# Fewer transfers for the same bytes: left slabs by two each, and both column halves of z by one

## The chip, the core and the metric

The kernel runs on one core of one Trainium2 chip. Its metric is device time in microseconds (us). The core has five engines that run side by side: TensorE (PE in the profile; PEld is its loading of weights), VectorE (DVE), ScalarE (ACT), GpSimd (POOL) and SyncE (SP), whose queue here issues nearly all DMA transfers. The transfers themselves are carried by 16 DMA engines that all queues share.

## The reference

An image x of 512 x 512 positions with 64 channels goes through two layers of the same form. A layer is

```
x = x + conv(groupnorm(x))               # 32 groups of 2 channels over the whole image

def conv(x):                             # DIM 64, HID 128, WIN 4, n = 512
    xn    = layernorm(x)
    left  = (xn @ Wl + bl) * mask * sigmoid(xn @ Wlg + blg)
    right = (xn @ Wr + br) * mask * sigmoid(xn @ Wrg + brg)
    gate  = sigmoid(xn @ Wog + bog)
    out   = sum over d in -4..4 of left[i, i + d] * right[i + d, j]     # for all j, per channel
    out   = layernorm(out) * gate
    return out @ Wo + bo
```

So `left` is needed only near the diagonal, in a band nine wide, and for each of the 128 channels the band times `right` is a banded matrix product along the rows. The second layer needs the group statistics of the whole first output.

## The kernel before

**Tiling.** The rows are cut in nine overlapping blocks of 64 (`S`, line 23; `row_blocks`, line 146), each with a halo of 4 rows. A block gives 56 finished rows, or 60 at the two edges of the image. The 512 columns are taken as two halves of 256 (`LH`, line 172) that are worked on together: partitions 0 to 63 hold the 64 rows at a column of the left half, partitions 64 to 127 the same rows at the matching column of the right half. A *unit* (class `Unit`, line 505) is 8 columns (`JU`) of each half, so its tile `z` has 128 partitions and 8 x 64 values, 2 KB a partition. Eight units make a chunk of 64 columns, four chunks a block: 36 chunks and 288 units in each layer.

**Stages of a unit.** `load` (line 514) brings z from the image. Two transfers do this, one for each column half (lines 520 and 521): 64 rows of 2 KB. GpSimd scales and moves it by the group norm (`scaled`, `moved`), VectorE takes the row statistics (`inner_stats`), GpSimd centres and rescales (`centred`, `rescaled`), TensorE turns it (`transposed`) and ScalarE keeps both turned copies. TensorE then projects to `right` and its gate; ScalarE and VectorE finish that into the tile RO. Once the eight units of a chunk are there, `mix` (line 720) multiplies the band matrices with RO, 16 channels at a time (`HA`, line 28). Sixteen units later (`LAG`) the second half of the work follows: statistics of the output, `norm` on GpSimd or ScalarE, turns and gates on TensorE, the product with Wo, the residual from tile XR, which `fetch` (line 876) loads again from the image, and `stored` (line 909). In the first layer the result goes to `mid_x` in HBM, in the second to the output.

**Left slabs.** The values near the diagonal are computed once a layer and lie in HBM. For each block `spread_left` (line 678) lays them out in `left_of`, again in HBM, as band matrices with zeros beside the band. `take_left` (line 706) brings one slab of them into the tile A: for one group `h` of 16 channels, 128 partitions of 8 x 128 values. It does so by four transfers of 128 KB: for each half `e` of the partitions two transfers of 4 x 512 B a partition. There are eight groups, and a slab is taken anew for every block, so 72 slabs a layer. Taking starts in the `load` step of a later unit, once the last chunk of the block before has used the slab (`on_copy`, line 1095, puts it in the list `slabs`; `on_load`, line 977, takes one from it).

**Order.** The order of the work is written out by hand in the tables FIRST (line 39) and SECOND (line 69), for the first and the second layer. A word such as `load:15` means: do the load step of unit 15, counted from the start of the period. One pass over the table is a period of eight units. Each engine gets its instructions in the order of the table and works through them in order (the class `InOrder`, line 488, is why the profile shows nearly everything at line 496). So the SP queue holds, in one line, the loads of z, the slabs of A, the fetches of XR, and the stores; an issue that waits holds up those behind it. z has 12 buffers (`NZ`, line 30), XR six. A load of z waits until the unit that used its buffer 12 units ago is turned. At the start of a layer 12 units are loaded ahead of the rest.

In SECOND the loads stand in bunches: `load:15`, `load:16`, `load:12` and `load:14` follow each other within four lines, and `load:19`, `load:17`, `load:18` within another four. Their `scale` steps come a few lines later. In FIRST they are spaced more evenly.

Of the kernel before, what the change touches and what calls it, by code (L numbers as in the profile page):

```python
# [20 lines left out]
WIN = 4  # L21
NEAR = 2 * WIN + 1
S = 64
JC = 64
JU = 8
JQ = 4
NU = JC // JU
HA = 16
# [130 lines left out]
def tile_two_banded_layers(  # L159
# [8 lines left out]
    H = layers[0]["Wl"].shape[1]  # L168
# [3 lines left out]
    LH = L // 2  # L172
# [15 lines left out]
    span = 2 * (S + 2 * WIN)  # L188
    size = S * H // 2 * span
    left_of = dram.tile([2, size], F32, name="left_of")  # L190
# [86 lines left out]
    def strided(v: bass.AP, at: int, *dims) -> bass.AP:  # L277

        return bass.AP(tensor=v.tensor, offset=v.offset + at, ap=[list(d) for d in dims])


    def fetch_layer(i: int, w: dict, tmp) -> dict:
# [9 lines left out]
        for e in range(2):  # L292
            part = slice(e * D, (e + 1) * D)
            for n, nm in enumerate(("r", "rg", "l", "lg", "og")):
                load(f["raw"][part, n * H : (n + 1) * H], w[f"W{nm}"])
            load(f["ns"][part], col(w["norm_scale"]))
            load(f["nb"][part], col(w["norm_bias"]))
# [207 lines left out]
    class Unit:  # L505
# [4 lines left out]
        def __init__(self, at: int, blk: Block = None, j: int = 0, near: int = None):  # L510
            self.at, self.blk, self.j, self.near = at, blk, j, near
            self.pr, self.sg, self.banks = {}, {}, {}

    def load(src: bass.AP, u: Unit):
        u.z = zp.tile([P, JU, D], F32, tag=f"z{u.at % NZ}", name="z")
        if u.near is not None:
            load_near(src, u)
            return
        rows = slice(u.blk.s, u.blk.s + S)
        for e, j in enumerate((u.j, LH + u.j)):  # L520
            en.sync.dma_start(u.z[e * S : (e + 1) * S], src[rows, j : j + JU, :])

    def load_near(src: bass.AP, u: Unit):
        spans = [(0, u.near, u.near + JU)]
        if u.near + JU > NEAR * JQ:
            spans = [(o, u.near, u.near + JQ) for o in range(0, JU, JQ)]
        for o0, n0, n1 in spans:
            for o, r, k, m in runs(n0, n1):
                z = u.z[:, o0 + o : o0 + o + m, :].rearrange("q m c -> q (m c)")
                at, q0, q1 = r * (L + 1) + k - WIN, 0, P  # L530
                pieces = []

                if r == 0 and k < WIN:
                    q0, g = 1, min(m, WIN - k)
                    pieces = [(0, 0, g, 0), (0, g, m, at + g)]
                if r == JQ - 1 and k + m > WIN + 1:
                    q1, g = P - 1, max(0, WIN + 1 - k)
                    end = (P - 1) * JQ * (L + 1) + at
                    pieces = [(P - 1, 0, g, end), (P - 1, g, m, L * L - m)]
                cut = [q0, *([16] if q0 else []), *([P - 16] if q1 < P else []), q1]  # L540
                for a0, a1 in sorted(zip(cut, cut[1:]), key=lambda c: c[0] - c[1]):
                    en.sync.dma_start(
                        z[a0:a1],
                        strided(
                            src, (a0 * JQ * (L + 1) + at) * D, (JQ * (L + 1) * D, a1 - a0),
                            (1, m * D),
                        ),
                    )
                for q, g0, g1, a in pieces:
                    if g0 < g1:  # L550
                        en.sync.dma_start(
                            z[q : q + 1, g0 * D : g1 * D],
                            strided(src, a * D, (D, 1), (1, (g1 - g0) * D)),
                        )
# [151 lines left out]
    def take_left(n: int, h: int):  # L706

        held[h] = n
        q = HA // 4
        for e in range(2):  # L710
            for k in range(2):
                en.sync.dma_start(
                    A[e * S : (e + 1) * S, h, k * q : (k + 1) * q].rearrange("p h i t -> p h (i t)"),
                    strided(
                        left_of, n % 2 * size + (h * HA // 2 + k * q) * span + 2 * WIN,
                        (H // 2 * span, S), (span, q), (1, 2 * S),
                    ),
                )

    def mix(c: int, h: int, b: str) -> tuple:  # L720

# [203 lines left out]
    def layer(src: bass.AP, dst: bass.AP, w: dict, stats: bool, then=None):  # L925
# [51 lines left out]
        def on_load(n, t, alt, b):  # L977
            if slabs:
                take_left(*slabs.pop(0))
            if t in units and t not in early:  # L980
                load(src, units[t])
# [106 lines left out]
        def on_band(n, t, alt, b):  # L1088
            if chunk(t):
                c, h = chunk(t)  # L1090
                while held.get(h) != c // per:
                    take_left(*slabs.pop(0))
                mixed[t] = mix(c, h, b)
# [141 lines left out]
    A = keep.tile([P, H // HA, HA // 2, S, 2], F32, name="A")  # L1235
# [38 lines left out]
def build(arrays):  # L1274
    import concourse.bacc as _bacc

    nc = _bacc.Bacc("TRN2", target_bir_lowering=False, num_devices=1)
    aps = {}
    for name in _INS:
        a = arrays[f"in_{name}_dram"]  # L1280
        aps[name] = nc.dram_tensor(
            f"in_{name}_dram", a.shape, mybir.dt.from_np(a.dtype), kind="ExternalInput"
        ).ap()
    out = nc.dram_tensor("out_0_dram", aps["x"].shape, F32, kind="ExternalOutput").ap()
    layers = [{n: aps[f"L{i}_conv_{n}"] for n in _NAMES} for i in range(2)]
    with tile.TileContext(nc) as tc:
        tile_two_banded_layers(tc, aps["x"], layers, out)
    return nc
# [10 lines left out]
```

## Time and profile before

| | us |
|---|---|
| median of 3 runs | 4308.89 |
| lowest and highest | 4305.12 and 4312.75 |
| profiled execution | 4288.38 |
| its span, first to last instruction | 4286.6 |

The profile is of one execution. Its page gives, for each engine, how long it was busy:

```profile
PE 3756.5 (88%) x94986; PEld 3258.3 (76%) x94986; DVE 3657.6 (85%) x9915; ACT 3181.7 (74%) x5976; POOL 3620.0 (84%) x4962
...
q1 hardware_dynamic: 692212, 580.43, 47.0%
```

The first line is busy time in us, its share of the span, and the count of instructions. The second is the DMA queue that SP feeds: packets, MB, and the time that its packets took as a share of 16 engines' span. A packet is one contiguous piece that a DMA engine moves, or a small record of a few bytes.

Other views are used below. The view of waits lists who waited for whom, with the total in us, the number of times and the longest one. The view of windows gives the busy time of each engine in a stretch of time, with the granted TensorE clock, the mean DMA share and GB/s. The timeline lists instructions in order of time: start and duration in us, the engine (SPq is SP's queue), what it writes and reads, and how many were merged into the row. In all of them "z<-mid_x" means that z is written from mid_x; "z<-z,ga" is the scaling of z.

### The profile page before, as it was taken

How to read it: one execution, taken by the hardware profiler on the slowest of the kernel's cores; microseconds unless marked ns; L12 is line 12 of the kernel's file. 1: busy time of each engine (PE TensorE's matmuls, PEld its weight loads, DVE VectorE, ACT ScalarE, POOL GpSimd, SP SyncE). 2: the span in 40 equal slices, each digit the busy share in tenths (PEclk: the TensorE clock that was granted, in tenths of full speed). 3: DMA queues.
4: the chain of work that ended last, by engine and by line, in shares of the span. 5: the costliest groups of instructions: out<-in, count | busy, mean ns of one | idle time of the engine just before them, and what ended most of it. 6: DMA issues, size and time to landing. Idle time of an engine off the chain costs nothing.

```text
span 4286.6 us, 223301 instructions
## 1 busy us (share of the span) xinstructions
PE 3756.5 (88%) x94986; PEld 3258.3 (76%) x94986; DVE 3657.6 (85%) x9915; ACT 3181.7 (74%) x5976; POOL 3620.0 (84%) x4962
## 2 busy tenths in 40 slices
PE   0169898989899999999995798999999999999998
PEld 0058787878788888888784687878878787878786
DVE  8988787878788888888877798989889898989897
ACT  0048787878787777878773687878888888989896
POOL 2389898989898989999855698998989898989893
PEclk9989999999999999999997899999999999999999
DMA  9843545454545444545434344444454545454533
GB/s 397 318 110 102 140 118 140 114 139 118 142 113 141 122 128 122 136 121 137 129 103 110 97 137 132 136 136 135 132 139 132 141 131 146 128 147 123 157 111 101
DMA packets 695719, 596.26 MB, mean 139 GB/s; under 512 B 138310, under 2 KB 549990, under 8 KB 692420
## 3 DMA queue, kind: packets, MB, share of 16 engines
q1 hardware_dynamic: 692212, 580.43, 47.0%
q8 instruction: 748, 12.26, 1.2%
q14 instruction: 247, 2.02, 0.2%
q0 software_dynamic: 2512, 1.56, 0.1%
HBM read 436.71 MB, written 149.74 MB: 137 GB/s over the span
## 4 chain that ended last, share of the span: by engine, by line
PE 58%; DVE 12%; POOL 9%; DMA 7%; SPq 6%; issue 5%; ACT 2%; DVEq 0%; POOLq 0%; ACTq 0%
PE banks L496 44%; PE bank L496 10%; POOL z L496 6%; SPq L496 6%; POOL on L496 3%; PE acc L496 3%; DVE sti L496 2%; DMA z<-in_x_dram 2%; DVE RO L496 2%; DVE sto L496 2%; DVE gn_st L496 2%; DMA z<-mid_x 2%; DVE XR L496 1%; DVE ZH L496 1%; ACT on L496 1%
## 5 line engine op out<-in xcount | busy, mean ns | idle before, releaser
L496 POOL TENSOR_SCALAR on<-RO,rs,nm 128x128 f32<-128x128 f32 x2520 | 1117.9, 456 | 193.3 <-PE banks L496 139.9
L496 ACT ACTIVATE on<-RO,nm,rs 128x128 f32<-128x128 f32 x2088 | 971.7, 499 | 108.4 <-PE banks L496 95.1
L496 PE MATMUL banks<-pack,ZT 64*128 64x128 f32 x9216 | 987.4, 287 | 24.4 <-DVE RO L496 15.3
L496 PE MATMUL banks<-pack,zT 64*128 64x128 f32 x9216 | 945.0, 279 | 2.2 <-issue 1.3
L496 POOL TENSOR_TENSOR z<-z,ga 128x512 f32<-128x512 f32 x556 | 649.8, 1175 | 301.9 <-DMA z<-in_x_dram 135.3
L496 ACT ACTIVATE sg<-banks 128x512 f32<-128x512 f32 x1170 | 696.1, 596 | 279.9 <-PE banks L496 253.8
L496 PEld LDWEIGHTS banks<-pack,ZT 64*128 64x128 f32 x9216 | 771.5, 194 | 148.4 <-DVE RO L496 49.6
L496 DVE TENSOR_TENSOR RO<-banks,sg 128x512 f32<-128x512 f32 x1152 | 777.6, 683 | 94.8 <-ACT sg L496 72.5
L496 DVE BATCH_NORM_STATS2 sto<-RO 128x6 f32<-128x256 f32 x2304 | 847.9, 413 | 6.7 <-ACT RO L496 2.6
L496 DVE SCALAR_TENSOR_TENSOR ZH<-banks,pack,ZH 128x896 f32<-128x896 f32 (+1 forms) x576 | 668.7, 1161 | 195.5 <-PE banks L496 163.2
L496 PEld LDWEIGHTS banks<-pack,zT 64*128 64x128 f32 x9216 | 754.0, 194 | 3.9 <-ACT zT L496 2.4
L496 PEld LDWEIGHTS banks<-RO,A 64*64 64x64 f32 x36864 | 617.2, 136 | 139.0 <-DVE RO L496 43.9
L496 PE MATMUL banks<-RO,A 64*64 64x64 f32 x36864 | 693.4, 223 | 32.3 <-issue 18.8
L496 PE MATMUL bank<-pack,ZH 128*64 128x64 f32 x18432 | 666.7, 226 | 12.5 <-DVE XR L496 5.6
L496 ACT COPY RO<-banks 128x1024 f32<-128x1024 f32 x540 | 540.2, 1008 | 173.6 <-PE banks L496 162.1
L496 POOL TENSOR_TENSOR z<-z,gb 128x512 f32<-128x512 f32 x556 | 651.5, 1177 | 3.3
L496 PEld LDWEIGHTS bank<-pack,ZH 128*64 128x64 f32 x18432 | 594.0, 139 | 72.9 <-issue 31.0
L496 ACT ACTIVATE ZH<-banks 128x896 f32<-128x896 f32 (+1 forms) x576 | 531.6, 929 | 135.2 <-PE banks L496 129.4
L496 POOL TENSOR_TENSOR z<-z,rs 128x512 f32<-128x512 f32 x586 | 611.9, 1053 | 20.9 <-DVE rs L496 20.5
L496 POOL TENSOR_TENSOR z<-z,sti 128x512 f32<-128x512 f32 x586 | 617.8, 1067 | 7.7 <-DVE sti L496 7.7
L496 PE MATMUL banks<-ZT,pack 64*128 64x448 f32 (+1 forms) x2304 | 587.3, 583 | 3.4 <-issue 1.2
L496 PE MATMUL banks<-ident,on 64*128 64x64 f32 x9216 | 461.7, 230 | 125.7 <-POOL on L496 119.3
(204 smaller groups left out, 4188.7 us busy)
## 6 DMA issues: line engine op xcount, KB each, us to landing
z<-in_x_dram SPq DMA_DIRECT2D x576, 128.0 KB
A<-left_of SPq DMA_DIRECT2D x576, 128.0 KB
z<-mid_x SPq DMA_DIRECT2D x576, 128.0 KB
gn_x<-in_x_dram SPq DMA_DIRECT2D x16, 4096.0 KB
XR<-in_x_dram SPq DMA_DIRECT2D x448, 112.0 KB
mid_x<-XR SPq DMA_DIRECT2D x448, 112.0 KB
XR<-mid_x SPq DMA_DIRECT2D x448, 112.0 KB
out_dram<-XR SPq DMA_DIRECT2D x448, 112.0 KB
```

What stands on the lines that cost most here:

```text
L496: return lambda *a, **k: tc.keep_in_program_order(f(*a, **k))
```

## The change

Two kinds of transfers are cut in fewer pieces. The bytes that are moved, where they come from and where they go stay the same, and so do all other instructions and the two tables.

```
+    def halves(v: bass.AP, j: int) -> bass.AP:
+
+        return v.rearrange("p (e l) c -> e p l c", e=2)[:, :, j : j + JU, :].rearrange(
+            "e p j c -> e p (j c)"
+        )
+
     def load(src: bass.AP, u: Unit):
...
         rows = slice(u.blk.s, u.blk.s + S)
-        for e, j in enumerate((u.j, LH + u.j)):
-            en.sync.dma_start(u.z[e * S : (e + 1) * S], src[rows, j : j + JU, :])
+        en.sync.dma_start(u.z, halves(src[rows], u.j))
...
     def take_left(n: int, h: int):
 
         held[h] = n
-        q = HA // 4
         for e in range(2):
-            for k in range(2):
-                en.sync.dma_start(
-                    A[e * S : (e + 1) * S, h, k * q : (k + 1) * q].rearrange("p h i t -> p h (i t)"),
-                    strided(
-                        left_of, n % 2 * size + (h * HA // 2 + k * q) * span + 2 * WIN,
-                        (H // 2 * span, S), (span, q), (1, 2 * S),
-                    ),
-                )
+            en.sync.dma_start(
+                A[e * S : (e + 1) * S, h].rearrange("p h i t -> p h (i t)"),
+                strided(
+                    left_of, n % 2 * size + h * HA // 2 * span + 2 * WIN,
+                    (H // 2 * span, S), (span, HA // 2), (1, 2 * S),
+                ),
+            )
```

For z, `halves` views the 64 rows of the image as an array of two column halves x 64 rows x 512 values, in that order of its dimensions, and one transfer of 256 KB writes all 128 partitions of the tile from it. Each layer has 288 of these in place of 576. The loads of the diagonal's own values (`load_near`) stay as they were.

For A, the two transfers of 4 x 512 B a partition become one of 8 x 512 B, for each half of the partitions: 144 transfers of 256 KB a layer in place of 288 of 128 KB.

## The prediction

> **What bounds the kernel now.** I read the page first, for the shares of the chain and the packets.
>
> ```profile
> span 4286.6 us, 223301 instructions
> ...
> DMA packets 695719, 596.26 MB, mean 139 GB/s; under 512 B 138310, under 2 KB 549990, under 8 KB 692420
> ...
> PE 58%; DVE 12%; POOL 9%; DMA 7%; SPq 6%; issue 5%; ACT 2%; DVEq 0%; POOLq 0%; ACTq 0%
> ```
>
> TensorE carries most of the chain that ends last; DMA and the SP queue together have 13%. The wait view then says which transfers are late.
>
> ```profile
> POOL z L496 <- DMA z<-in_x_dram: 135.3, 44, 6.7
> POOL z L496 <- DMA z<-mid_x: 114.5, 52, 10.8
> ```
>
> Columns: total us, times, longest. GpSimd scales every z after its load, and 96 of 576 loads are waited for already. So z has little spare time before its use, and a later landing is paid at once. No row of that view has TensorE waiting for A. Last I read the stretches of the input statistics and of the two layers, with the DMA share (mean of the 16 engines) and GB/s in the last two columns.
>
> ```profile
> core 0: us, PE busy (x) PEld busy (x) DVE busy (x) ACT busy (x) POOL busy (x), PEclk, DMA share, GB/s
> 0.00:150.00 150.00, 18.81 (x36) 9.26 (x36) 131.14 (x417) 1.28 (x1) 55.50 (x133) 1.00 0.96 383
> 266.00:2190.00 1924.00, 1794.33 (x47296) 1582.62 (x47298) 1597.71 (x4301) 1493.60 (x2752) 1735.71 (x2379) 0.97 0.47 126
> 2350.00:4200.00 1850.00, 1740.18 (x43682) 1509.12 (x43684) 1639.27 (x4376) 1542.30 (x2955) 1663.35 (x2196) 0.97 0.46 133
> ```
>
> In both layers TensorE is busy 93 to 94% of the time and GpSimd 90%; the 16 DMA engines less than half. As a whole, DMA is no bound. The question is whether it stays spread over 16 engines.
>
> **How transfers are spread.** The packets tell.
>
> ```profile
> z<-in_x_dram SPq DMA_DIRECT2D x576, 128.0 KB
> A<-left_of SPq DMA_DIRECT2D x576, 128.0 KB
> z<-mid_x SPq DMA_DIRECT2D x576, 128.0 KB
> ...
> XR<-in_x_dram SPq DMA_DIRECT2D x448, 112.0 KB
> mid_x<-XR SPq DMA_DIRECT2D x448, 112.0 KB
> XR<-mid_x SPq DMA_DIRECT2D x448, 112.0 KB
> out_dram<-XR SPq DMA_DIRECT2D x448, 112.0 KB
> XR<-in_x_dram SPq DMA_DIRECT2D x128, 120.0 KB
> mid_x<-XR SPq DMA_DIRECT2D x128, 120.0 KB
> XR<-mid_x SPq DMA_DIRECT2D x128, 120.0 KB
> out_dram<-XR SPq DMA_DIRECT2D x128, 120.0 KB
> ...
> left_of<-left_rows SPq DMA_DIRECT2D x64, 72.0 KB
> left_of<-A SPq DMA_DIRECT2D x8, 72.0 KB
> ```
>
> Of the 138310 packets under 512 B, the 72 slab spreads explain 72 x 1024 = 73728 (72 KB in runs of 72 B). The other 64582 are far more than there are transfers; I read them as one closing packet for each engine that took part. If every transfer used 16 engines, the rows above alone would need (1728 + 1792 + 512 + 72) x 16 = 65664: too many. If the engines taken are the largest number up to 16 that divides the leading count of the transfer (14 for 56 rows, 15 for 60, 16 for 64 or 16), they need 27648 + 25088 + 7680 + 1152 = 61568, and 3014 are left for the rarer transfers. The second fits. So here the leading count decides how many engines work on a transfer.
>
> **The change, part by part.** *z.* Today each half load leads with 64 rows on both sides: 16 engines, 4 rows of 2 KB each. The new transfer writes 128 partitions, but its source is read as 2 halves x 64 rows x 2 KB: it leads with 2. Two engines is the only count over 1 that divides both 2 and 128. I forecast that each z runs on two engines, the same two each time, 131072 B on each. No row of before shows a transfer whose two sides lead with such different counts, so this is the step that can fall. [...]
>
> Price of one z on such an engine: in the first 150 us the engines stream at 383 / (16 x 0.96) = 24.9 GB/s, which gives 5.26 us; in the second layer a busy engine moves 133 / (16 x 0.46) = 18.1 GB/s and in the first 126 / (16 x 0.47) = 16.8, which give 7.24 and 7.80 us. A mean over short transfers holds their starts; 64 rows in one go are nearer to the stream. I take 5.26 and keep 7.24 and 7.80 as the other end.
>
> The same two engines still carry a sixteenth of everything else. First layer: 0.47 x 1924 = 904 us busy, less z's 288 x 16384 B at 16.8 GB/s = 281, leaves 623 us, 2.16 us a unit (288 units). Second: 0.46 x 1850 = 851 less 261 leaves 590, 2.05 a unit. So each of the two needs 7.42 and 7.31 us a unit, where the layers now take 1924/288 = 6.68 and 1850/288 = 6.42. **The floor** of the loss, were the two never idle, is 0.74 x 288 + 0.89 x 288 = 213 + 256 = 469 us: 4758 for this execution.
>
> They are idle at times, as the loads come in bunches. The SP queue in one period (8 units) of the second layer:
>
> ```profile
> 3045.73 6.28 SPq L496 DMA_DIRECT2D z<-mid_x  x8
> ...
> 3057.25 1.09 SPq L496 DMA_DIRECT2D z<-mid_x  x2
> ...
> 3059.48 3.38 SPq L496 DMA_DIRECT2D z<-mid_x  x4
> ...
> 3083.12 1.75 SPq L496 DMA_DIRECT2D z<-mid_x  x2
> ```
>
> and GpSimd's first use of them:
>
> ```profile
> 3050.54 2.33 POOL L496 TENSOR_TENSOR z<-z,ga 128x512 f32<-128x512 f32 x2
> 3055.48 1.16 POOL L496 TENSOR_TENSOR z<-z,ga 128x512 f32<-128x512 f32 x1 [0.84 <-DMA z<-mid_x]
> 3073.21 1.17 POOL L496 TENSOR_TENSOR z<-z,ga 128x512 f32<-128x512 f32 x1
> ```
>
> Eight half loads (units 15, 16, 12, 14 of the table) go out from 3045.73, two (unit 19) at 3057.25, four (17, 18) at 3059.48: seven units within 17 us. On two engines they need 7 x 7.31 = 51.2 us, to 3096.9. Unit 18 is wanted at 3073.21, so GpSimd comes 23.7 us late; unit 14, fourth of the bunch, is wanted at 3055.48 and lands at 3045.73 + 29.2 = 3074.9. GpSimd works in order, and behind a stalled scaling stand its norms, for which TensorE's turns wait, so the period stretches. TensorE's idle 6% of a 51 us period (8 x 6.42) can take back 3 us. Net 21 x 36 periods = +756. What follows a bunch is one load, so no backlog passes on.
>
> The first layer issues its loads more evenly; there I take the floor, 8 x 0.74 = 5.9 a period, and half a load, 2.6, for idle spells: 8.5 x 36 = +306. The 12 loads ahead of each layer take 12 x 5.26 = 63 us on two engines, partly beside other work: +15 each, between 0 and 60. Sum: 4288 (span 4286.6 and what lies around it) + 306 + 756 + 30 = 5380.
>
> *A.* Each slab half is now one transfer of 64 rows x 8 x 512 B instead of two: it still leads with 64, 16 engines. The price of an issue:
>
> ```profile
> L496 SPq DMA_DIRECT2D z<-in_x_dram x592: 246/588/1962, 166.9 to 2136.8; - x198
> L496 SPq DMA_DIRECT2D A<-left_of x576: 573/614/1848, 254.4 to 4057.6; - x192
> ```
>
> (ns: shortest, median, longest.) 288 A issues fewer at 614 and 576 z issues fewer at 588 take 177 + 339 = 516 us off SP. Where z is late that buys nothing, since SP then waits as well; I count 0, between 0 and the chain's SPq share, 6% or 257 us. A slab lands later behind z on two engines, but it is loaded a chunk ahead of its use: nothing.
>
> The median run is 0.48% above the profiled one: 5380 x 1.0048 = 5406, so **5400 us**.
>
> **The rivals.**
> *Dear packets and a blocked queue.* At 7.80 us a z the first layer needs 9.96 a unit, +3.28 x 288 = 945; at 7.24 the second needs 7 x 9.29 = 65.0 a bunch, 37.5 late less 3, x 36 = 1242; with 30 that is 6505, as a median 6540. For it: busy engines show that rate now, and SP waits for transfers to land:
>
> ```profile
> SPq L496 <- DMA mid_x<-XR: 207.2, 137, 3.6
> ```
>
> so a slow z can hold the stores and fetches queued behind it. Against it: that rate is one of short pieces beside 15 other busy engines.
>
> *Two engines, but another pair each time.* Then no engine is overfull and only the landing is later, by 5.26 less 0.66 (16 KB at 24.9) = 4.6 us. Paid once a bunch in the second layer (36 x 4.6 = 166) and at each of the 44 waits of the first (202): 4309 + 368 = 4680. Nothing in the profile shows how engines are picked.
>
> *The transfer is dealt by its 128 destination partitions*, 16 engines as now. This ends on the other side: one issue less ahead of the landing, 0.59 us at each of 96 waits, 57 us, gives 4250; it decides wherever the source's leading 2 doesn't count. Against it: the spread of packets above follows the leading count, and 2 can't be cut in 16. [...]
>
> *No effect*, because z has time: the 96 waits speak against it.
>
> **How the numbers follow.** Forecast, two fixed engines near 5.3 us: 0.64. Dear packets: 0.19. Changing pair: 0.06. Sixteen engines: 0.09, of which 0.07 faster and 0.02 within the bound. No effect: 0.02. The range goes from the floor (4758 x 1.0048 = 4780) up to 6250, three quarters of the way to the dear case, and leaves out the sixteen engines, no effect, the pair case and about half of the dear one: some 2 in 10. A measurement of this kernel can tell about 0.2% from no change. Faster 0.07, same 0.04, slower 0.89.
>
> **What would show it.** With two engines, z's closing packets fall from 1152 x 16 to 576 x 2 and A's lose 288 x 16, so the hardware queue's packets fall by 17280 + 4608 = 21888; with sixteen for z only by 9216 + 4608 = 13824. GpSimd's waits for z grow from 250 us to about a thousand, TensorE's wait for GpSimd with them, most in the second layer; the mean DMA share falls below 0.4 although two engines are full. GpSimd's and TensorE's busy times stay. If z's waits shrink, the two-engine step is wrong; if they grow by under 469 us, the pairs change or an engine is faster than 24.9 GB/s.

## The result and the profile after

The changed kernel takes 5794.96 us (median of 4 runs, 5786.81 to 5802.83), the kernel before 4310.82 us beside it. The ratio is 1.344, with a 95% interval of 1.340 to 1.347: slower by 34%. The forecast was 5400 us, with a range of 4780 to 6250.

The page of the changed kernel, its lines on busy time, the DMA queue and the chain that ended last:

```profile
span 5801.1 us, 221803 instructions
...
PE 4067.7 (70%) x94986; PEld 3486.6 (60%) x94986; DVE 3691.0 (64%) x9915; ACT 3202.2 (55%) x5976; POOL 3624.2 (62%) x4962
...
q1 hardware_dynamic: 670324, 580.34, 34.5%
...
PE 28%; DMA 23%; POOL 21%; issue 13%; SPq 7%; DVE 6%; ACT 2%; POOLq 0%; DVEq 0%; ACTq 0%
```

GpSimd, VectorE and ScalarE do the same work in the same busy time, in a span that is a third longer. DMA has gone from 7 to 23% of the chain, GpSimd from 9 to 21%. Yet the queue's packets keep 16 engines busy only 34.5% of the time, where they had 47.0%: less DMA work at once, and more waiting for it.

The hardware queue has 670324 packets where it had 692212: 21888 fewer, which is what two engines for z give (18432 - 1152 closing packets less) with A's 4608. They are all under 512 B: the page counts 138310 packets of that size before and 116422 after. Sixteen engines for z would have left 678388.

A window shows the two engines themselves. Between 197 and 215 us little but loads ahead of the first layer is under way (columns as before; the last two are DMA share and GB/s):

```profile
197.00:215.00 18.00, 1.37 (x4) 1.00 (x4) 16.21 (x63) 0.00 (x0) 0.86 (x1) 1.00 0.13 49
```

0.13 of 16 is two engines on the mean, and 49 GB/s is 24.5 GB/s on each. So 131072 B take 5.35 us, where nothing else moves. The landings in the trace agree: each z leaves two landing marks after one at its issue, and four z have their last mark at 203.52, 208.87, 214.21 and 219.57, 5.34 to 5.36 us apart.

The view of waits, after, and below it the row on XR of the kernel before:

```profile
POOL z L496 <- DMA z<-mid_x: 900.4, 165, 31.8
POOL z L496 <- DMA z<-in_x_dram: 840.4, 164, 14.5
...
DVE XR L496 <- DMA XR<-mid_x: 542.4, 34, 26.0
```

```profile
DVE XR L496 <- DMA XR<-mid_x: 74.1, 11, 10.6
```

GpSimd's waits for z have gone from 250 to 1741 us, by 1491; the kernel lost 1484. XR, whose transfers were not changed, is waited for 542 us where it was 74. Its 56 or 60 rows are spread over 14 or 15 engines (as many landing marks a transfer, after one at its issue). I read it to have shares on the same two: of the 14 marks of the fetch issued at 1514.69 us, twelve came 2.0 to 2.5 us after the issue, the last two after 8.87 and 9.27 us, at 1523.56 and 1523.96; the z issued ahead of it, at 1509.83, had landed at 1522.17.

Where the time went by stages is read from the first and the last transfer of a kind. First the kernel before, then the changed one, in the view of the tile mid_x (issue in ns, then first and last start in us):

```profile
L496 SPq DMA_DIRECT2D mid_x<-XR x576: 307/436/1802, 342.3 to 2294.4; - x192
L496 SPq DMA_DIRECT2D XR<-mid_x x576: 306/394/2266, 2416.5 to 4271.0; - x192
```

```profile
L496 SPq DMA_DIRECT2D mid_x<-XR x576: 313/448/5048, 400.3 to 3025.8; - x192
L496 SPq DMA_DIRECT2D XR<-mid_x x576: 306/392/5890, 3193.8 to 5787.4; - x192
```

The first layer's stores took 1952 us and now take 2626: +673. The second layer's fetches took 1855 and now take 2594: +739. The start lost 58 us and the passage between the layers 46.

### The profile page after: what moved, and what is told of

It is laid out like the page before. It is cut to its first block, busy times and chain, and to the rows that moved or that the text cites. A ratio compares the mean times of both kernels' runs of the same rounds, so it can differ in the third digit from the quotient of the medians.

```text
span 5801.1 us, 221803 instructions
## 1 busy us (share of the span) xinstructions
PE 4067.7 (70%) x94986; PEld 3486.6 (60%) x94986; DVE 3691.0 (64%) x9915; ACT 3202.2 (55%) x5976; POOL 3624.2 (62%) x4962
## 2 busy tenths in 40 slices
DMA packets 673820, 596.08 MB, mean 103 GB/s; under 512 B 116422, under 2 KB 528102, under 8 KB 670532
## 3 DMA queue, kind: packets, MB, share of 16 engines
q1 hardware_dynamic: 670324, 580.34, 34.5%
## 4 chain that ended last, share of the span: by engine, by line
PE 28%; DMA 23%; POOL 21%; issue 13%; SPq 7%; DVE 6%; ACT 2%; POOLq 0%; DVEq 0%; ACTq 0%
PE banks L496 21%; POOL z L496 14%; DMA z<-mid_x 11%; DMA z<-in_x_dram 8%; SPq L496 7%; POOL on L496 7%; PE bank L496 5%; PE acc L496 2%; DVE gn_st L496 1%; DMA mid_x<-XR 1%; DVE ZH L496 1%; DVE RO L496 1%; ACT on L496 1%; ACT RO L496 1%; DVE XR L496 0%
## 5 line engine op out<-in xcount | busy, mean ns | idle before, releaser
L496 POOL TENSOR_TENSOR z<-z,ga 128x512 f32<-128x512 f32 x556 | 650.4, 1170 | 1823.2 <-DMA z<-mid_x 900.4
L496 PE MATMUL banks<-ident,on 64*128 64x64 f32 x9216 | 541.5, 243 | 845.4 <-POOL on L496 839.5
L496 PE MATMUL banks<-pack,ZT 64*128 64x128 f32 x9216 | 1056.5, 301 | 108.0 <-DVE RO L496 98.4
L496 PEld LDWEIGHTS banks<-ident,on 64*128 64x128 f32 x9216 | 427.6, 150 | 972.8 <-POOL on L496 911.3
L496 PE MATMUL banks<-pack,zT 64*128 64x128 f32 x9216 | 1002.9, 290 | 2.5 <-issue 1.6
L496 PEld LDWEIGHTS banks<-pack,ZT 64*128 64x128 f32 x9216 | 841.0, 208 | 239.6 <-DVE RO L496 120.2
L496 DVE TENSOR_TENSOR XR<-bank,XR 120x512 f32<-120x512 f32 (+1 forms) x576 | 391.9, 680 | 813.5 <-DMA XR<-mid_x 542.4
L496 PEld LDWEIGHTS banks<-pack,zT 64*128 64x128 f32 x9216 | 812.6, 206 | 2.9 <-ACT zT L496 2.1
L496 DVE BATCH_NORM_STATS2 sti<-z 128x6 f32<-128x128 f32 x2344 | 505.7, 281 | 459.5 <-POOL z L496 456.7
L496 PE MATMUL bank<-pack,ZH 128*64 128x64 f32 x18432 | 723.6, 237 | 34.3 <-DVE XR L496 25.5
L496 PEld LDWEIGHTS bank<-pack,ZH 128*64 128x64 f32 x18432 | 648.1, 150 | 97.3 <-issue 32.9
```

Of the source, the lines that this page charges most:

```text
L496: return lambda *a, **k: tc.keep_in_program_order(f(*a, **k))
```

## The experiments

All kernels are held against the kernel before, run beside them in five groups (4286 to 4311 us). Between kernels of different groups, differences under some 25 us say nothing. The three that lead with 128, 8 and 4 bring as many bytes in runs of 2 KB, but to other partitions or from other columns, so they don't compute the layer. A table first; the waits are GpSimd's for z, both layers, and the last column is the mean granted TensorE clock of the profiled run.

| kernel | z's engines | us | ratio to before (95%) | waits for z, us | clock |
|---|---|---|---|---|---|
| before | 16, two transfers | 4311 | 1 | 250 | 0.965 |
| changed | 2 | 5795 | 1.344 (1.340 to 1.347) | 1741 | 0.860 |
| z alone | 2 | 5777 | 1.346 (1.344 to 1.349) | 1664 | 0.858 |
| A alone | 16, two transfers | 4224 | 0.985 (0.983 to 0.986) | 185 | 0.975 |
| leads with 128 | 16 | 4221 | 0.984 (0.982 to 0.986) | 167 | 0.975 |
| leads with 8 | 8 | 4383 | 1.022 (1.020 to 1.023) | 305 | 0.963 |
| leads with 4 | 4 | 4727 | 1.103 (1.099 to 1.107) | 663 | 0.935 |
| every other unit | 2 or 16 | 4931 | 1.149 (1.147 to 1.152) | 846 | 0.922 |
| loads moved up | 2 | 5658 | 1.319 (1.317 to 1.321) | 1090 | 0.868 |
| A alone, loads moved up | 16, two transfers | 4389 | 1.022 (1.020 to 1.025) | 95 | 0.965 |
| z from ScalarE's queue | 2 | 6496 | 1.516 (1.513 to 1.518) | 2344 | 0.830 |
| the same with two transfers | 16 | 4583 | 1.069 (1.068 to 1.071) | 447 | 0.968 |
| spare load on two engines | 16, spare 2 | 6209 | 1.444 (1.440 to 1.447) | 1979 | 0.835 |
| spare load on 16 engines | 16, spare 16 | 4581 | 1.065 (1.062 to 1.068) | 446 | 0.942 |

### The two parts alone

z by one transfer, with A's four left as they were:

```
     def take_left(n: int, h: int):
...
+        q = HA // 4
         for e in range(2):
+            for k in range(2):
...
```

> z by one transfer, A by four as before. Theory (z's transfer leads with 2 and runs on two fixed engines, all of the loss is there): 5750 to 5850, and the hardware queue's packets are 670324 + 4608 = 674932. Rival (the larger slabs of A, which stand in SP's queue behind z, carry a good part): under 5500.

Measured: 5776.54 us and 674932 packets, as the theory had it. The whole loss is z's part.

A by two, with z's two transfers left:

```
-        en.sync.dma_start(u.z, halves(src[rows], u.j))
+        for e, j in enumerate((u.j, LH + u.j)):
+            en.sync.dma_start(u.z[e * S : (e + 1) * S], src[rows, j : j + JU, :])
```

> A by two transfers each, z by two as before. Theory: A still leads with 64, 16 engines; 288 issues fewer save SP at most 288 x 0.61 = 177 us of its own time, most of it hidden: 4270 to 4315. Rival (larger slabs hold up the queue): over 4350. Packets 692212 - 4608 = 687604 in both.

Measured: 4224.19 us, better than expected: 1.5% faster than before, and 687604 packets. The waits of this kernel:

```profile
POOL z L496 <- DMA z<-mid_x: 95.7, 38, 10.1
POOL z L496 <- DMA z<-in_x_dram: 89.6, 44, 4.5
```

They fell by 65 us, and the time by 66. In SP's queue a slab's issues stand ahead of the load that follows (before, four issues of A at 3005.45 took 2.58 us ahead of the z of 3008.14); with two of them z goes out earlier; that is how I read the two equal numbers. This kernel beats both others.

### One transfer on 16 engines

The same single transfer, with its source as one dimension of 128 rows:

```
-        return v.rearrange("p (e l) c -> e p l c", e=2)[:, :, j : j + JU, :].rearrange(
-            "e p j c -> e p (j c)"
-        )
+        return v.rearrange("p (e l) c -> (p e) l c", e=2)[:, j : j + JU, :].rearrange(
+            "q j c -> q (j c)"
+        )
```

> The change, but z's one transfer reads its source as 128 rows in one dimension (row and column half interleaved on the partitions, so the halves' rows do not lie where the rest of the kernel wants them; the same bytes of HBM are read, and all else is as in the changed kernel). Theory (the leading count sets the engines): 16 engines again, 4230 to 4320. Rival (one transfer of 256 KB in place of two is slow by its size or its single landing): 5500 to 5850. Packets with 16 engines: 692212 - 9216 - 4608 = 678388.

Measured: 4220.80 us, 678388 packets. One transfer of 256 KB with one landing costs nothing; the leading count costs 34%. It also gains nothing over two transfers (4224): 576 issues fewer on SP buy 3 us, which is within the spread of the runs (4219 to 4227).

### The count of engines

```
-        return v.rearrange("p (e l) c -> e p l c", e=2)[:, :, j : j + JU, :].rearrange(
+        return v.rearrange("p (e l) c -> e p l c", e=4)[:, :, j : j + JU, :].rearrange(
...
-        en.sync.dma_start(u.z, halves(src[rows], u.j))
+        rows = slice(u.blk.s, u.blk.s + P // 4)
+        en.sync.dma_start(u.z, halves(src[rows], u.j % (L // 4)))
```

> The change, but z's one transfer leads with 4 (a quarter of the columns x 32 rows for each quarter of the partitions: the same count of bytes, other positions of the image than the kernel wants, so the output differs). Four engines: 32 rows of 2 KB on each, 2.7 us, and 2.7 + 2.2 = 4.9 us a unit on them. Theory (engines follow the leading count; landing late by 2.0 us against 4.7 with two engines): 4300 to 4600. Rival (anything but the count of engines, such as a source in several dimensions, makes z slow): over 5500.

> As with 4, but leading with 8: eighths of the columns x 16 rows. Eight engines, 1.3 us, 0.7 us later than with 16: 4220 to 4280, within 1.5% of the kernel that leads with 128 rows (4221). Packets of the hardware queue: 678388 less 576 x 8 = 673780.

(The kernel that leads with 8 has 8 in the three places of the 4.)

Measured: 4727.02 us with 4 (671476 packets) and 4382.73 us with 8 (673780). The engines follow the leading count, but the size was missed: 506 and 162 us over the kernel that leads with 128, where at most 380 and 60 had been expected. With 8 engines each is held only 1.3 us a z by estimate (a quarter of 5.35), and with the rest (2.05 to 2.16 by the prediction's estimate) they have 3.5 us of work in the 6.4 to 6.7 us that a unit took before. So the loss doesn't begin where engines are full on the mean; it grows with the time that a z holds its engines (5.35 us measured, 2.7, 1.34 and 0.67 by estimate as its half, quarter and eighth, give 1574, 506, 162 and 0).

### Half of the units

```
+        if u.at % 2 == 0:
+            en.sync.dma_start(u.z, halves(src[rows], u.j))
+            return
+        for e, j in enumerate((u.j, LH + u.j)):
+            en.sync.dma_start(u.z[e * S : (e + 1) * S], src[rows, j : j + JU, :])
-        en.sync.dma_start(u.z, halves(src[rows], u.j))
```

> The change for units of even number only; odd units load z by two transfers; A by two. The two engines then carry 5.35 + 0.66 + 2 x 2.2 = 10.4 us for two units, 5.2 a unit, under the 6.4 to 7.0 that the layers took before. Theory that the two engines are overfull (throughput): under a third of the loss stays, 4400 to 4750. Rival (each such load costs its own late landing, however full the engines are): half of the loss stays, 4950 to 5150.

Measured: 4930.85 us, 707 over A's part alone, 45% of the changed kernel's 1571. That is outside both expectations, 19 us under the rival's range and 181 above the other's: near a half and far from a third. Engines that are full on the mean are not what the loss is, then: each such load has its price even when the two have time to spare (by the estimate above 5.2 of 6.4 us or more a unit). What it is paid for, the load's own lateness or the two engines being taken, was still open.

### Earlier loads

```
+    steps = [s for s in steps if s[0] != "load"]
+    turns = [(n, s[2]) for n, s in enumerate(steps) if s[0] == "ztr"]
+    for n, at in reversed(turns):
+        steps.insert(n + 9, ("load", 0, at + NZ, False, ""))
     return steps
```

> The changed kernel with every load step moved up in both tables to nine steps behind the turn that frees its buffer. Theory (the loss is late landing: the loads are issued about a unit ahead, and the two engines stand idle between them): much of the loss goes, down towards the floor of two full engines, 4760 to 5200, and GpSimd's waits for z, 1741 us, fall by half or more. Rival (the two engines are full already, or SP is held up whatever the order): over 5600.

> z by two transfers, A by two, and the load steps moved up as in the other kernel. Theory (z's landing is waited for a little in every kernel, 250 us of GpSimd's waits before): 4120 to 4220, faster than A's part alone (4224). Rival (those waits are covered elsewhere, or a load that waits on SP for its buffer holds up stores and fetches): 4220 to 4300.

Measured: 5658.37 us, 137 less than the changed kernel (some 106 by the ratios, as the groups differ), on the rival's side; and with 16 engines 4389.12 us, slower than without the move and outside both expectations. The waits of the first of them (line 500 here is line 496 elsewhere):

```profile
POOL z L500 <- DMA z<-mid_x: 662.7, 62, 32.8
DVE XR L500 <- DMA XR<-mid_x: 627.8, 92, 23.5
...
DVE XR L500 <- DMA XR<-in_x_dram: 538.2, 113, 23.3
...
POOL z L500 <- DMA z<-in_x_dram: 427.6, 118, 13.2
```

GpSimd waits 651 us less for z, and VectorE waits 1166 us for XR, where it was some 600 in the changed kernel. I read this as lateness that is handed on: whoever is first on the two engines makes the others late. The kernel with 16 engines became slower by 165 us, while VectorE's waits for XR rose from 58 to 219 us. The view of SP's own waits of this kernel shows a second cost of moving up:

```profile
SPq L500 <- PE banks L500: 1121.3, 379, 13.1
```

SP now stands before a load whose buffer TensorE still has to free (339 us with A alone), and stores and fetches stand behind it.

### Another queue

```
-        en.sync.dma_start(u.z, halves(src[rows], u.j))
+        en.scalar.dma_start(u.z, halves(src[rows], u.j))
```

> The changed kernel with z's one transfer issued from ScalarE's queue instead of SP's. It still leads with 2. Theory (the loss is a queue's: on the two engines every store, fetch and slab stands behind a z of 5.3 us, SP is held at its full queue, and so the next loads go out late): the queues share the two engines, SP is held less, and half or more of the loss goes: 4700 to 5250. Rival (z's own 5.3 us on two engines, as GpSimd sees it, is the loss, whichever queue it comes from): 5550 to 5850. ScalarE pays the issues itself, some 0.5 x 576 = 300 us in a kernel in which it is busy 55%; its control is the run beside it.

> Control: z by two transfers (16 engines), A by two, z issued from ScalarE's queue. 1152 issues of about 0.5 us on ScalarE, busy 75%: 4230 to 4450, against 4224 from SP's queue. It tells how much of the other run's time is ScalarE's own.

Measured: 6496.25 us, outside both expectations, and 4583.12 us for its control, above its expectation too: issuing from ScalarE costs 359 us by itself. Taking z off SP's queue makes it worse: 1913 us over its control, where from SP's queue it was 1571.

```profile
POOL z L496 <- DMA z<-in_x_dram: 1259.4, 169, 15.4
POOL z L496 <- DMA z<-mid_x: 1085.1, 146, 31.4
...
DVE XR L496 <- DMA XR<-mid_x: 121.8, 23, 18.0
```

XR is now waited for 122 us in place of 542, and z 2344 in place of 1741. I read it so: with a queue of its own z no longer stands ahead of the fetches; it shares the two engines with them and is later itself. The order within SP's queue thus decides who waits here. The loss doesn't need z in that queue.

Here z is alone on its queue (q10), first with one transfer, then with two:

```profile
q10 hardware_dynamic: 74880, 151.00, 6.7%
```

```profile
q10 hardware_dynamic: 92160, 151.07, 11.9%
```

74880 is 576 x (128 + 2), 92160 is 576 x 128 + 1152 x 16: the pieces of 2 KB, and one closing packet for each engine. The share gives an estimate of the price within the layers too: 6.7% of 16 engines' 6492.8 us is 6.0 us on each of two engines a z, against 5.35 where nothing else moved. It is 12.1 us of engine time a z, where two transfers on 16 engines took 15.1 (11.9% of 16 engines' 4580.2 us).

### The two engines taken by a load that nobody reads

z on 16 engines, and behind it a further load of the same shape on two:

```
+        d = zp.tile([P, JU, D], F32, tag=f"d{u.at % 2}", name="d")
+        en.sync.dma_start(d, halves(src[rows], u.j))
```

> A by two, z by two transfers on 16 engines, and behind them, for every unit, a further transfer of the same 256 KB that leads with 2 into a spare tile that nobody reads. It puts 5.35 us a unit on the same two engines as the change does (7.5 us a unit with the rest, and 0.7 of z's own), but z itself isn't on it. Theory that z's own late landing at GpSimd is the loss: z waits for a spare of another unit only where two loads follow closely: 4250 to 4650. Rival (the two engines as such are the loss: whatever stands behind, stores, fetches, the next unit's z, comes 5 us late): 5200 to 5900.

> Control: the same spare bytes by two transfers that lead with 64, 16 engines. 0.67 us a unit on each engine and 1152 more issues on SP at 0.59, 680 us of a queue that waits half of its time: 4224 to 4450.

Measured: 6209.09 us, and 4580.93 us for the control with the same spare bytes on 16 engines: +1628. Both lie above their expectations; the first is on the rival's side and beyond its figure. Waits of the kernel with the spare load on two engines:

```profile
POOL z L496 <- DMA z<-in_x_dram: 991.4, 145, 18.3
POOL z L496 <- DMA z<-mid_x: 988.0, 157, 38.6
...
DVE XR L496 <- DMA XR<-mid_x: 845.7, 62, 30.2
DVE XR L496 <- DMA XR<-in_x_dram: 440.3, 87, 32.5
```

z itself is loaded as in A's part alone here (two transfers on 16 engines each, 687604 packets there), and is waited for more than in the changed kernel. So the loss doesn't need z on two engines. But the spare has only two buffers, so it brings a wait of its own: SP waits until an earlier spare has landed before it may issue the next one, and all that stands behind waits along. SP's waits that a spare's landing ends:

```profile
SPq L496 <- DMA d<-mid_x: 795.9, 173, 9.7
...
SPq L496 <- DMA d<-in_x_dram: 166.0, 98, 8.3
```

In the control they are 61.5 and 0.7 us. The first layer (in_x_dram), with few such waits, is the cleaner test; its stores with the spare on two engines, then on 16:

```profile
L496 SPq DMA_DIRECT2D mid_x<-XR x576: 313/436/4816, 417.0 to 3192.2; - x192
```

```profile
L496 SPq DMA_DIRECT2D mid_x<-XR x576: 307/436/2060, 347.2 to 2382.8; - x192
```

That is 2775 us against 2036, +740, with 166 us of these waits. The explanation that fits is that two engines are taken for 5.35 us a unit: every transfer that stands behind them in SP's queue and is spread over 16 engines has a share on those two, and is landed only when they are through with it, as the two late marks of the XR fetch showed in the changed kernel. How much of the 1628 us is this and how much is SP being held was not separated.

## Why the prediction was right or wrong

**The spread follows the leading count.** Right, and shown by the packets (670324, to the packet), the window of two busy engines, and the kernels that lead with 4, 8 and 128. The step that the trace of before couldn't settle, a source and a tile that lead with different counts (2 and 128), goes by a count that divides both in each of the four kernels: 2, 4, 8 and 128 beside 128 gave 2, 4, 8 and 16 closing packets a z. Also z alone on ScalarE's queue has one closing packet for each of two engines (74880). That the pair is the same two each time was the author's assumption; the trace of before couldn't show it. No view here names the engine of a packet, but the window above bears it out: SP had further loads to issue there, some three were under way, and the mean was two busy engines. The z issued at 187.22, 187.92, 188.88 and 193.36 landed one after the other, at 196.98, 203.52, 208.87 and 214.21; on different pairs they could have run side by side.

**The price.** 5.26 us forecast from the rate of long streams, 5.35 measured where nothing else moved, and some 6.0 as the estimate within the layers of the kernel that loads z from ScalarE's queue. Right in the main; the dear packets of the rival (7.24 to 7.80) were not there.

**The second layer, +756.** Measured +739. One period of it, SP's loads and the scalings that waited:

```profile
4377.52 9.48 SPq L496 DMA_DIRECT2D z<-mid_x  x4
...
4403.82 0.50 SPq L496 DMA_DIRECT2D z<-mid_x  x1
...
4405.32 4.23 SPq L496 DMA_DIRECT2D z<-mid_x  x2
```

```profile
4390.91 1.16 POOL L496 TENSOR_TENSOR z<-z,ga 128x512 f32<-128x512 f32 x1 [7.37 <-DMA z<-mid_x]
...
4396.86 1.15 POOL L496 TENSOR_TENSOR z<-z,ga 128x512 f32<-128x512 f32 x1 [4.80 <-DMA z<-mid_x]
...
4402.05 1.15 POOL L496 TENSOR_TENSOR z<-z,ga 128x512 f32<-128x512 f32 x1 [3.60 <-DMA z<-mid_x]
...
4412.44 1.17 POOL L496 TENSOR_TENSOR z<-z,ga 128x512 f32<-128x512 f32 x1 [1.98 <-DMA z<-mid_x]
...
4424.01 1.16 POOL L496 TENSOR_TENSOR z<-z,ga 128x512 f32<-128x512 f32 x1 [2.80 <-DMA z<-mid_x]
```

The last of the seven (unit 18) has landed when its scaling starts at 4424.01, 46.5 us after the bunch began, where 51.2 were forecast. The five waits are 20.6 us together; 21 net were forecast. So the bunch works as worked out, only the lateness is spread over five scalings, and SP needs 32 us to issue the seven loads, not 17.

**The first layer, +306: this term failed.** Measured +673. The forecast said that it "issues its loads more evenly; there I take the floor", plus half a load for idle spells. From the chain of the changed kernel, in the first layer, one row of each period of 8 units (start, duration):

```profile
905.23 12.77 DMA z<-in_x_dram
...
977.32 11.74 DMA z<-in_x_dram
...
1047.68 12.21 DMA z<-in_x_dram
...
1121.54 11.28 DMA z<-in_x_dram
...
1208.72 12.62 DMA z<-in_x_dram
```

From 905.23 to 1208.72 are 303.5 us for 32 units: 9.5 us a unit. By estimate the two engines have 5.35 + 2.16 = 7.5 us of work in it (8.2 with the 6.0 above), so they are idle for a seventh to a fifth of the time, and the floor says little. The reason can be read in the timelines of SP, GpSimd and VectorE. SP first:

```profile
1523.21 0.56 SPq L496 DMA_DIRECT2D z<-in_x_dram  x1
1523.82 4.88 SPq L496 DMA_DIRECT2D XR<-in_x_dram  x4
1537.57 0.78 SPq L496 DMA_DIRECT2D mid_x<-XR  x2
1538.46 5.14 SPq L496 DMA_DIRECT2D z<-in_x_dram  x2
```

GpSimd in the same stretch:

```profile
1522.24 1.17 POOL L496 TENSOR_TENSOR z<-z,ga 128x512 f32<-128x512 f32 x1 [3.30 <-DMA z<-in_x_dram]
...
1533.78 1.15 POOL L496 TENSOR_TENSOR z<-z,ga 128x512 f32<-128x512 f32 x1 [8.38 <-DMA z<-in_x_dram]
1534.89 1.15 POOL L496 TENSOR_TENSOR z<-z,gb 128x512 f32<-128x512 f32 x1
```

and VectorE's next two rows:

```profile
1536.07 0.88 DVE L496 BATCH_NORM_STATS2 sti<-z 128x6 f32<-128x128 f32 x4 [8.70 <-POOL z L496]
1536.87 0.67 DVE L496 TENSOR_TENSOR XR<-bank,XR 120x512 f32<-120x512 f32 x1
```

The load of 1523.21 is used at 1533.78, after GpSimd has waited 8.38 us for it. The moving of a z at 1534.89 stands behind that scaling in GpSimd's order, and VectorE's statistics have waited 8.70 us for it and start at 1536.07. Behind them in VectorE's order stands the addition of an earlier unit's result to XR, at 1536.87; SP stores such an XR at 1537.57, right as the addition ends, before it can issue the next load at 1538.46. So from the landing near 1533.7 until then the two engines have no z. It is a loop: a late z makes results late, late results hold SP, and SP issues the next z late. I worked out how much the two engines can carry, and not how long the loop around them is. The loop is read from these rows; the experiments bear it out in part (earlier loads shorten it for z and lengthen it for XR), but no run isolates it. SP is also held by the stores of this layer: it fetches into a buffer of XR only when the store from it has landed, and these waits grew from 207.2 to 698.5 us. How the 673 us divide among z, XR and SP stays open.

**The start, +30 for both layers' first loads.** Measured 58 and 46, each within the bounds of 0 to 60, but 104 together: this term was too small by 74 us. That the time came out within the range doesn't make the sum right: for the profiled execution it gave 5380 us against 5802.83, 423 short, by these 74 and the first layer's 367, with 17 too many in the second.

**A, 0.** Right beside a slow z: 5795 with A's part and 5777 without. By itself the part is worth 66 us, within the bounds of 0 to 257 that the chain's share gave.

**What was to show it.** GpSimd's waits were to grow to about a thousand us, most of it in the second layer: they grew to 1741, almost even between the layers (840.4 and 900.4), which is the same error as the first layer's term. TensorE's weight loads waited 911.3 us for GpSimd's norms, where it was 149.7, as forecast in kind. The DMA share fell below 0.4 as forecast. GpSimd's busy time stayed; TensorE's didn't (3756 to 4068), see below.

**The rivals.** Sixteen engines is out, by the packets. "Another pair each time" is out by the window of two busy engines, "no effect" by the time. The blocked queue, put down to dear packets, was right in that SP is held and wrong in its price. SP's waits for stores, 207.2 us before, are in the changed kernel:

```profile
SPq L496 <- DMA mid_x<-XR: 698.5, 139, 7.8
```

## What to carry to other kernels

Look at the outermost dimension of both sides of a transfer before two are merged into one: here a leading dimension of 2 put all of each z on two engines, and the closing packets in the DMA count told it at once (74880 on z's own queue, 92160 with two transfers on 16). A transfer on few engines can be paid by others that have a share on those engines, as XR (542 us of waits where it was 74), and by the queue behind it (SP waited 698.5 us for stores where it was 207.2); a mean DMA share of 34.5% hid it. And where loads go out only a unit or two ahead of their use, price a later landing by the wait of the engine that uses it: here, the growth of GpSimd's waits for z, 1491 us, was as large as the loss, 1484.

## What was not expected

**Time follows GpSimd's waits for z.** Against A's part alone, GpSimd's waits for z and the kernel's time grew by 120 and 159 us with 8 engines, 478 and 503 with 4, 661 and 707 with every other unit, 1556 and 1571 with the changed kernel. It fails where the loads are moved up, as the wait then goes to XR.

**SP is held while it issues.** The issues of z in the view of the tile z, after (shortest, median, longest in ns; the prediction has the row of before):

```profile
L496 SPq DMA_DIRECT2D z<-in_x_dram x304: 246/534/7403, 167.9 to 2842.0; - x152
```

7.4 us where it was 1.96. Eight of them took 29.25 us from 186.89; the last five took 27.27 from 188.88, 5.45 each, which is about the 5.35 that two engines need for a z. These five issues ended at 193.32, 199.72, 203.43, 210.88 and 216.15, each time with three or four z issued and not landed. I read it so: SP's next issue is held by the z that wait on the two engines; no view shows how. There is a second hold, which the trace shows in the semaphores: each of SP's 3295 transfers tells its landing by the semaphore that the one eight before it used, and SP waits at issues until a z has landed: 217.5 us in all (170.7 for z from mid_x, 46.8 for z from the input), 1.8 before. Fewer issues had been meant to be less work for SP; SP was held longer.

**TensorE's granted clock was lower where it waited more.** The same 94986 matmuls were busy 3756 us before and 4068 after, at a granted clock of 0.965 and 0.860, while the weight loads' waits for GpSimd's norms went from 149.7 to 911.3 us; over the runs the clock mostly goes down as the time goes up, from 0.975 at 4221 us to 0.830 at 6496 (an exception is 0.968 at 4583). So a late load seems to make TensorE's own work slower as well. What the clock goes by was not shown, and how much of the loss is the clock's was not tried.
